# A four-layer vision block in one pass: layers and experts as two rows of pieces beside the scan, experts one at a time with their sum in DRAM, one PSUM ring for all

## The chip, the cores and the metric

The kernel runs on one core of a Trainium2 chip. The metric is the device time of one launch in microseconds (us); three runs of the kernel before gave 5811.77, 5817.92 and 5828.28 us, median 5817.92. The engines are called as in the profile: PE (TensorE, matmuls), PEld (its weight loads), DVE (VectorE), ACT (ScalarE), POOL (GpSimd) and SP (SyncE, which issues nearly all DMAs here).

## What is computed

The input `x` is 4 images of 384 channels by 48x48 positions, fp32. Four residual layers follow each other, each on a group-normalised input:

```
x = x + L0(_gn(x))   # Mamba block: projections, a 4-tap conv, a scan over 2304 positions
                     # with 768 channels x 16 states, gate, output projection, layer norm
x = x + L1(_gn(x))   # 1x1 projection, 8x8 FFT filter, 3x3 depthwise conv, gated GELU, 1x1 projection
x = x + L2(_gn(x))   # depthwise 11x11 convolution
x = x + L3(_gn(x))   # 4 experts (384->384->384, ReLU), outputs weighted by a coefficient per expert
```

In the last layer the coefficient of every expert is 1 for the given data unless some expert is never chosen. So the kernel sums all four experts unweighted, checks at the end, and recomputes with weights only if the check fails. This fallback (`weighted`) does not run here.

## The kernel before

**The scan.** `scans` is a generator. It walks 4 images (`b`) times 5 chunks (`t`) of 460 or 464 positions times 96 units (`q`), 1920 units in all. One unit handles 128 channels and one of the 16 states: ACT makes the decay `da` (L627, an Exp into PSUM), POOL makes `bu` (L631), DVE runs the recurrence (L635), DVE or POOL multiplies by the state's output row into `g` (L642), and PE turns `g` and adds it up in PSUM as `y` (L591). The output rows `bc` are broadcast from DRAM by an SP DMA for every second unit, into four buffers. The projections, the conv and the end of a chunk are planned at fixed units and take their PSUM tiles from `bank` of `scans`.

**Work beside the scan.** While image `b` is scanned, two lists of small closures, each with a weight, are worked off after every `yield`. `later(b - 1, bg)` is layers 1 to 3's gate scores of the previous image: layer 1 in strips (`patches`, `spectrum`, `taps`, `gelu`, `value`, `project1`), layer 2 by channel tile (`load2`, `blocks`, `windows`, `finish_band`), then `scores_of`. `experts(b - 2, pool, bg)` is layer 3 of the image before that. They stand in one queue, experts first, and a share of weight per unit is spent on it, so that it ends with the image.

**After the scan** there is a last part without a scan ("the tail" below): `later` of image 3, with the experts of image 2 interleaved piece by piece, then the routing (`route_all`), then the experts of image 3 alone.

**Experts.** `begin(e)` loads both weight matrices of an expert and scales the first; all four stay in SBUF. `biases` makes the bias corrections of all four. The steps go strip by strip (16 strips of 144 positions), and in a strip expert by expert, 64 per image. `hidden(s, e)` is 9 matmuls into PSUM (`ph`, L1142) and three ReLUs on ACT (`hr`, L1150); `output` is 9 matmuls (`pout`, L1160). `output` of step i-1 is placed behind `hidden` of step i. All four experts of a strip add up in one PSUM tile; DVE adds the input and the bias sum (L1171) and SP stores the strip.

**PSUM.** 8 banks. In the scan part: 2 for `bank` of `scans` (tag `mm`), 2 for `da`, 2 for `y`, and 2 single ones for the work beside it, tag `B` for nearly everything and `A` for sums that stay open (`dw`, `pc`, `pout`).

**Order.** Instructions are put in each engine's queue by a scheduler at build time, which takes them by their place in the program and by when it reckons them ready. On the chip each queue is worked off in order.

Of the kernel before, what the change touches and what calls it, by code (L numbers as in the profile page):

```python
# [16 lines left out]
P = 128  # L17
# [27 lines left out]
def tile_layers(ctx: ExitStack, tc: tile.TileContext, a: dict, out: bass.AP):  # L45
# [75 lines left out]
    def route_all(rt, bg):  # L121
# [44 lines left out]
        ps = bg.tile([P, 512], F32, name="pseen", tag="B")  # L166
# [97 lines left out]
    with ExitStack() as first:  # L264
# [55 lines left out]
        stats0 = wp.tile([P, NB, CT, 2, 3, 6], F32, name="stats0")  # L320
# [69 lines left out]
        stats1 = [wp.tile([P, CT, NC, 6], F32, name=f"stats1_{b}") for b in range(NB)]  # L390
        stats2 = [wp.tile([P, CT, NLB, 6], F32, name=f"stats2_{b}") for b in range(NB)]
        stats3 = [wp.tile([P, CT, len(BANDS), 6], F32, name=f"stats3_{b}") for b in range(NB)]
# [18 lines left out]
        def scans(wk, mm):  # L411


            def bank(name):
                return mm.tile([P, 512], F32, name=name, tag="mm")
# [5 lines left out]
            def image_stats(b, ct, h):  # L421
# [3 lines left out]
                for k in range(3):  # L425
                    nc.vector.bn_stats(stats0[:, b, ct, h, k, :], t[:, bass.ts(k, LB)])

            def image_norm(b):
                group_norm(
                    stats0[:, b].rearrange("p c h k s -> p c (h k) s"), bank,  # L430
                    mean0[:, b], rstd0[:, b], f"0_{b}",
                )
# [269 lines left out]
            def residual(i, ct):  # L702
# [14 lines left out]
                nc.vector.bn_stats(stats1[b][:, ct, t, :], x)  # L717
# [67 lines left out]
        def later(b, bg):  # L785
# [5 lines left out]
            def bank(name, tag="B"):  # L791
                return bg.tile([P, 512], F32, name=name, tag=tag)


            def begin1():
# [8 lines left out]
                group_norm(stats1[b], bank, mean, rstd, f"1_{b}")  # L804
# [27 lines left out]
            def patches(hb, wb):  # L832
# [10 lines left out]
                ts_ = d["ts"] = d["wk"].tile([P, C], F32, name=f"tp{u_}", tag="tp")  # L843
                nc.scalar.copy(ts_, ps[:, :C])

            def spectrum(hb, wb):
# [3 lines left out]
                us = d["wk"].tile([P, C], F32, name=f"uf{u_}", tag="uf")  # L850
# [21 lines left out]
            def taps(hb, ct):  # L872

                acc = d["acc", ct] = bank(f"dw{b}_{hb}_{ct}", "A")
# [11 lines left out]
            def gelu(hb, ct):  # L886
                if ct == 0:
                    d["act"] = d["wk"].tile([P, 2, LB], F32, name=f"act{b}_{hb}", tag="act")
# [13 lines left out]
            def project1(hb, ct):  # L902
# [11 lines left out]
                nc.vector.bn_stats(stats2[b][:, ct, hb, :], x)  # L914
# [31 lines left out]
            def begin2():  # L946
# [4 lines left out]
                group_norm(stats2[b], bank, mean, rstd, f"2_{b}")  # L951
# [11 lines left out]
            def load2(ct):  # L963
                x = d["x2", ct] = d["wk"].tile([P, HW], F32, name=f"x2_{b}_{ct}", tag="x2")
# [27 lines left out]
            def windows(ct, k, r, first, last):  # L992

                if first:
                    d["acc2"] = bank(f"pc{b}_{ct}_{k}", "A")
# [20 lines left out]
            def finish_band(ct, k):  # L1016
# [3 lines left out]
                nc.vector.bn_stats(stats3[b][:, ct, k, :], x)  # L1020
# [4 lines left out]
            work.append((1, lambda: load2(0)))  # L1025
# [331 lines left out]
```

## Time and profile before

| what | us |
|---|---|
| median of three runs | 5817.92 |
| profiled execution, its own time | 5822.38 |
| its span | 5820.6 |
| scan of image 0 (nothing beside it), first to next image's first unit | 981 |
| scan of image 1 (later) | 1171 |
| scan of image 2 (experts, then later) | 1352 |
| scan of image 3 (experts, then later) | 1322 |
| from the last scan instruction to the end of the span | 902 |

The four scan rows are the times between the first scan instructions (L635) of two images in the trace; image 3's ends with its last one. Busy time of an engine is the sum of its instructions' durations as the profiler shows them, merged where they overlap in the tables of stretches. PEclk is the share of full clock that PE was granted. The page's mean clock is 0.88.

### The profile page before, as it was taken

The numbers are of one execution on the slowest core, as the hardware profiler recorded it, in microseconds if no ns is written. First come the engines' busy times: TensorE is split into PE (matmuls) and PEld (weight loads), VectorE is DVE, ScalarE is ACT, GpSimd is POOL, SyncE is SP. The second block draws the span as 40 slices with busy tenths as digits, with TensorE's granted clock in tenths as the row PEclk, the third lists the DMA queues.
The fourth block names the chain that finished last, engine by engine and source line by source line (L and its number), as shares of the span: only waits on it lengthen the run. The fifth ranks groups of instructions, "written<-read, shape, count | busy, mean of one in ns | idle before, by whom it ended". The sixth has DMA issues, their size and how long they took to land. (4 is left out here: it accounts for less than half of the span.)

```text
span 5820.6 us, 78509 instructions
## 1 busy us (share of the span) xinstructions
PE 4897.0 (84%) x27796; PEld 3787.9 (65%) x27796; DVE 4014.5 (69%) x5653; ACT 3053.3 (52%) x6658; POOL 3110.4 (53%) x2795
## 2 busy tenths in 40 slices
PE   6677667778778898999867798999967698899999
PEld 3544444544456665889544676789744486789999
DVE  5888878889888787767788678666788767451110
ACT  3555555555566665555555576555555575345321
POOL 3877877765657677646464457555554556000000
PEclk9688778878789898999978699899978699899999
DMA  4344334333334335334333235333332334311100
GB/s 135 124 132 133 123 124 134 126 106 117 103 128 140 108 126 177 125 97 123 108 107 106 90 125 180 98 102 115 112 101 91 106 109 131 113 36 47 57 22 26
DMA packets 396048, 634.78 MB, mean 109 GB/s; under 512 B 32373, under 2 KB 386789, under 8 KB 392190
## 3 DMA queue, kind: packets, MB, share of 16 engines
q1 hardware_dynamic: 382148, 618.58, 33.5%
q10 hardware_dynamic: 13498, 11.11, 0.6%
q8 instruction: 220, 3.60, 0.3%
q14 instruction: 182, 1.49, 0.1%
HBM read 571.80 MB, written 57.80 MB: 108 GB/s over the span
## 5 line engine op out<-in xcount | busy, mean ns | idle before, releaser
L631 POOL TENSOR_TENSOR bu<-u,bc 128x460 f32<-128x460 f32 (+1 forms) x1920 | 2217.5, 1168 | 1348.8 <-DVE g L635 748.0
L591 PE MATMUL y<-ident,g 128*115 128x128 f32 (+1 forms) x7680 | 1346.3, 316 | 637.2 <-POOL g L642 539.8
L591 PEld LDWEIGHTS y<-ident,g 128*115 128x115 f32 (+1 forms) x7680 | 1110.5, 199 | 998.7 <-POOL g L642 686.2
L627 ACT ACTIVATE da<-dt,a_neg 128x460 f32<-128x460 f32 (+1 forms) x1920 | 1220.8, 645 | 667.3 <-DVE g L642 585.2
L635 DVE TENSOR_TENSOR_SCAN da<-da,carry,bu 128x460 f32<-128x460 f32 (+1 forms) x1008 | 1160.6, 1170 | 194.7 <-ACT da L627 155.6
L642 POOL TENSOR_TENSOR g<-g,bc 128x460 f32<-128x460 f32 (+1 forms) x660 | 765.9, 1160 | 268.2 <-DVE g L635 127.3
L642 DVE TENSOR_TENSOR g<-da,bc 128x460 f32<-128x460 f32 (+1 forms) x1260 | 771.1, 626 | 159.8 <-ACT carry L640 85.4
L635 DVE TENSOR_TENSOR_SCAN g<-da,carry,bu 128x460 f32<-128x460 f32 (+1 forms) x528 | 616.9, 1168 | 150.4 <-PE y L591 65.3
L1142 PE MATMUL ph<-xe,w 128*128 128x144 f32 x4608 | 624.8, 289 | 4.4 <-ACT hr L1150 3.9
L1160 PE MATMUL pout<-hr,w 128*128 128x144 f32 x4608 | 616.1, 287 | 0.0
L1142 PEld LDWEIGHTS ph<-xe,w 128*128 128x128 f32 x4608 | 591.1, 192 | 24.9 <-issue 10.9
L1160 PEld LDWEIGHTS pout<-hr,w 128*128 128x128 f32 x4608 | 584.8, 190 | 14.8 <-issue 7.9
L1001 PE MATMUL pc<-band,row 128*128 128x162 f32 (+14 forms) x3456 | 506.3, 297 | 3.8 <-DVE x L1019 3.5
L1001 PEld LDWEIGHTS pc<-band,row 128*128 128x128 f32 x3456 | 478.5, 205 | 20.9 <-DVE x L1019 6.9
L640 ACT COPY carry<-da 128x1 f32<-128x1 f32 x1008 | 158.7, 159 | 581.0 <-DVE da L635 575.9
L1150 ACT ACTIVATE hr<-ph,nb 128x144 f32<-128x144 f32 x768 | 235.6, 377 | 409.8 <-PE ph L1142 409.7
L881 DVE SCALAR_TENSOR_TENSOR dw<-pad,w_dw,dw 128x384 f32<-128x384 f32 x576 | 342.5, 610 | 12.9 <-ACT pad L869 9.3
L673 PE MATMUL po<-w_out,zs 128*115 128x384 f32 (+1 forms) x960 | 344.2, 500 | 4.3 <-DVE xc L504 3.5
L635 DVE TENSOR_TENSOR_SCAN da<-da,nil,bu 128x460 f32<-128x460 f32 x252 | 289.4, 1168 | 83.2 <-ACT da L627 65.9
L487 PE MATMUL pin<-xch,w_inx 128*128 128x463 f32 (+2 forms) x720 | 329.7, 586 | 7.6 <-DVE dt L582 5.4
L515 PE MATMUL pinz<-xch,w_inz 128*128 128x460 f32 (+1 forms) x720 | 317.9, 574 | 16.0 <-DVE xc L504 7.3
L1171 DVE SCALAR_TENSOR_TENSOR xe<-pout,b_sum,xe 128x144 f32<-128x144 f32 x192 | 58.7, 359 | 340.3 <-PE pout L1160 340.3
(173 smaller groups left out, 5355.6 us busy)
## 6 DMA issues: line engine op xcount, KB each, us to landing
bc<-bcd SPq DMA_DIRECT2D x768, 460.0 KB, 3.7
bc<-bcd SPq DMA_DIRECT2D x192, 464.0 KB, 3.6
xs<-x1d SPq DMA_DIRECT2D x24, 576.0 KB, 4.1
x2d<-xs SPq DMA_DIRECT2D x24, 576.0 KB, 3.0
x<-x2d SPq DMA_DIRECT2D x12, 1152.0 KB, 8.8
x3d<-x SPq DMA_DIRECT2D x12, 1152.0 KB, 4.6
xg<-x3d SPq DMA_DIRECT2D x24, 576.0 KB, 3.9
xe<-x3d SPq DMA_DIRECT2D x64, 216.0 KB, 2.6
```

The costliest lines, as they stand in the source:

```text
L487: nc.tensor.matmul(ps[:, lo : halo + n], lhsT=w_inx[:, k, bass.ts(j, P)], rhs=c["x"][:, k, lo : halo + n], start=k == 0, stop=k == CT - 1,)
L515: nc.tensor.matmul(ps[:, :n], lhsT=w_inz[:, k, bass.ts(j, P)], rhs=c["x"][:, k, DCONV - 1 : DCONV - 1 + n], start=k == 0, stop=k == CT - 1,)
L591: nc.tensor.matmul(y[:w, bass.ts(k, P)], lhsT=src[:, bass.ts(k, w)], rhs=ident, is_transpose=True, start=start and k == 0, stop=stop, skip ...
L627: nc.scalar.activation(da[:, :n], c["dt", p][:, m % 2, :n], AF.Exp, scale=a_neg[:, m, s : s + 1])
L631: nc.gpsimd.tensor_mul(bu[:, :n], c["u", p][:, m % 2, :n], bc[:, 0, :n])
L635: nc.vector.tensor_tensor_scan(here[:, :n], da[:, :n], bu[:, :n], last if t else nil[:, 0:1], ALU.mult, ALU.add,)
L642: eng.tensor_mul(g[:, :n], here[:, :n], bc[:, 1, :n])
L673: nc.tensor.matmul(ps[:w, :C], lhsT=c["zs"][:, m, bass.ts(k, w)], rhs=w_out0[:, m, :], start=m == 0, stop=m == MT - 1,)
L881: nc.vector.scalar_tensor_tensor(v, src, w_dw[:, ct, k : k + 1], v, ALU.mult, ALU.add)
L1001: nc.tensor.matmul(d["acc2"][:, : BANDS[k] * W].rearrange("p (h w) -> p h w", w=W)[:, lo - edges[k] : hi - edges[k], xlo:xhi], lhsT=d["row ...
L1142: nc.tensor.matmul(ps[:, bass.ts(m, EB)], lhsT=d["w1"][:, e, k, bass.ts(m, P)], rhs=d["x", s][:, k, :], start=k == 0, stop=k == CT - 1,)
L1160: nc.tensor.matmul(d["o"][:, bass.ts(m, EB)], lhsT=d["w2"][:, e, k, bass.ts(m, P)], rhs=d["h", s, e][:, k, :], start=e == 0 and m == 0 and ...
```

## The change

- **Two rows of pieces.** `later(b - 1)` is now worked off alone in the first three quarters of image `b`'s scan. When it is through, it appends `experts(b - 1)` to a second list, `two`, which is worked off at its own rate of one image's experts per image of scan. So experts start a quarter of a scan earlier, and run beside the layers of the next image instead of before them.
- **Experts one by one.** The loop is now expert by expert, and in an expert strip by strip. One expert's weights are in SBUF at a time (`bufs=1`), and its bias correction is made in `begin`. The sum over experts lies in a DRAM tensor `y3d`: expert 0 writes input, bias sum and its output there, experts 1 and 2 load the strip, add and store it, expert 3 loads it, adds and stores to `out`. The input strip is loaded again for each expert. `output(s, e)` now follows `hidden(s, e)` at once in the program, and `hr` has one buffer in place of three.
- **One PSUM ring.** `bank` of `scans`, of `later` and of `experts`, and now `pout` too, share one tag `mm` with 3 buffers in the scan part (6 in the tail); the open sums `dw` and `pc` have `acc` with 1 (2 in the tail).
- **Smaller buffers.** `tp`, `uf`, `act` and the layer-2 image tile `x2` go from 2 buffers to 1, and `load2` of the next channel tile is no longer issued ahead. Statistics are kept for 2 images in place of 4.

```diff
@@ experts: one at a time, sum in DRAM
+            y3d = dram.tile([C, HW], F32, name=f"y3d{b}")
...
+                w1 = d["w1"] = wk.tile([P, CT, C], F32, name=f"w1_{b}_{e}", tag="w1", bufs=1)
+                w2 = d["w2"] = wk.tile([P, CT, C], F32, name=f"w2_{b}_{e}", tag="w2", bufs=1)
...
+            def load3(s, e):
+                x = d["x", s, e] = wk.tile([P, CT, EB], F32, name=f"xe{b}_{s}_{e}", tag="xe")
                 nc.sync.dma_start(x, strip(x3d[b], bass.ts(s, EB)))
+                if e:
+                    y = d["y", s, e] = wk.tile([P, CT, EB], F32, name=f"ye{b}_{s}_{e}", tag="ye")
+                    nc.sync.dma_start(y, strip(y3d, bass.ts(s, EB)))
...
+                h = d["h"] = wk.tile([P, CT, EB], F32, name=f"hr{b}_{s}_{e}", tag="hr", bufs=1)
...
+                if e:
+                    y = d["y", s, e].rearrange("p c t -> p (c t)")
+                    nc.vector.tensor_add(y, ps[:, : CT * EB], y)
+                    to = strip(out[b] if e == NE - 1 else y3d, bass.ts(s, EB))
+                    nc.sync.dma_start(to, d["y", s, e])
+                    return
...
-            steps = [(s, e) for s in range(HW // EB) for e in range(NE)]
-            for i, (s, e) in enumerate(steps):
-                if e == 1 and s + 1 < HW // EB:
-                    work.append((0.2, lambda s=s: load3(s + 1)))
-                work.append((2.2, lambda s=s, e=e: hidden(s, e)))
-                if i:
-                    work.append((2.2, lambda i=i: output(*steps[i - 1])))
-            work.append((2.2, lambda: output(*steps[-1])))
+            for e in range(NE):
+                work.append((4, lambda e=e: begin(e)))
+                work.append((0.1, lambda e=e: load3(0, e)))
+                for s in range(NS):
+                    if s + 1 < NS:
+                        work.append((0.1, lambda s=s, e=e: load3(s + 1, e)))
+                    work.append((2.2, lambda s=s, e=e: hidden(s, e)))
+                    work.append((2.2, lambda s=s, e=e: output(s, e)))
@@ the scan part: two rows
+            banks[:] = mm, {"mm": 3, "acc": 1}
+            one, share, share2 = [], 0.0, 0.0
+            states = 2 * DS * (MT // 2) * NC
+            rate2 = None
             for b, t, q in scans(wk, mm):
                 at = 2 * DS * (MT // 2) * t + q
                 if b and at == 24:
+                    one, share = later(b - 1, banks), 0.0
+                    one.append((0, lambda b=b: two.extend(experts(b - 1, ew, banks))))
+                    rate = sum(w for w, _ in one) / (0.75 * (states - at))
+                share = run(one, share + rate) if one else 0.0
+                if two:
+                    rate2 = rate2 or sum(w for w, _ in two) / states
+                    share2 = run(two, share2 + rate2)
@@ the tail
+            banks[:] = mm, {"mm": 6, "acc": 2}
+            one, share = later(NB - 1, banks), 0.0
+            rate = sum(w for w, _ in two) / sum(w for w, _ in one)
+            for w, piece in one:
+                piece()
+                share = run(two, share + w * rate)
+            run(two, 1e9)
+            coef, whole = route_all(rt, mm)
+            run(experts(NB - 1, ew, banks), 1e9)
@@ layer 2: one image tile
-                x = d["x2", ct] = d["wk"].tile([P, HW], F32, name=f"x2_{b}_{ct}", tag="x2")
+                x = d["x2", ct] = d["wk"].tile([P, HW], F32, name=f"x2_{b}_{ct}", tag="x2", bufs=1)
...
-            work.append((1, lambda: load2(0)))
             for ct in range(CT):
-                if ct + 1 < CT:
-                    work.append((1, lambda ct=ct: load2(ct + 1)))
+                work.append((1, lambda ct=ct: load2(ct)))
```

`run(queue, share)` takes pieces from the front of a list as long as the share of weight covers the first one, and gives back what is left.

## The prediction

> **What bounds the kernel now.** I read first the busy shares, then the table of stretches cut where one kind of work beside the scan ends and the next begins, then the timeline of the tail.
>
> ```profile
> PE 4897.0 (84%) x27796; PEld 3787.9 (65%) x27796; DVE 4014.5 (69%) x5653; ACT 3053.3 (52%) x6658; POOL 3110.4 (53%) x2795
> ...
> 100.00:1074.00 974.00, 680.98 (x2903) 466.26 (x2902) 820.18 (x1022) 526.09 (x1115) 764.25 (x680) 0.78 0.41 128
> 1152.00:1657.00 505.00, 380.97 (x1490) 238.51 (x1489) 442.10 (x637) 275.56 (x575) 302.18 (x273) 0.81 0.36 109
> 1675.00:2180.00 505.00, 432.67 (x2452) 338.24 (x2453) 398.80 (x507) 334.69 (x728) 360.31 (x320) 0.88 0.39 128
> 2288.00:2788.00 500.00, 485.13 (x3454) 432.68 (x3453) 338.50 (x445) 264.68 (x662) 299.50 (x266) 0.98 0.36 111
> 2788.00:3253.00 465.00, 339.63 (x1326) 210.57 (x1325) 382.10 (x566) 243.51 (x491) 243.02 (x223) 0.81 0.34 105
> 3273.00:3561.00 288.00, 267.41 (x1746) 222.51 (x1745) 202.39 (x263) 205.24 (x413) 173.31 (x154) 0.93 0.35 116
> 4962.00:5240.00 278.00, 269.23 (x1677) 227.60 (x1678) 128.31 (x254) 107.62 (x220) 1.73 (x10) 0.94 0.23 75
> 5240.00:5500.00 260.00, 259.67 (x2122) 253.33 (x2123) 31.02 (x76) 123.57 (x310) 1.07 (x2) 1.00 0.14 47
> 5500.00:5821.00 321.00, 314.85 (x2476) 305.42 (x2474) 31.84 (x110) 63.91 (x203) 0.00 (x0) 0.98 0.11 31
> ```
>
> Columns: stretch, length, busy PE, PEld, DVE, ACT, POOL, PE's granted clock, DMA share, GB/s. In order: scan alone (image 0), layer 1 and layer 2 beside image 1's scan, experts, layer 1 and layer 2 beside image 2's scan, and the tail's three parts. Alone and under layer 1 the scan is bound by DVE (84%, 88%, 82%); under experts by PE (97%, DVE only 68%); under layer 2 mostly by PE (93%). The tail is PE from end to end. No row has both at 90%.
>
> ```profile
> 5600.80 2.37 PE L1142 MATMUL ph<-xe,w 128*128 128x144 f32 x18
> 5602.89 2.27 PEld L1160 LDWEIGHTS pout<-hr,w 128*128 128x128 f32 x18
> 5603.01 2.37 PE L1160 MATMUL pout<-hr,w 128*128 128x144 f32 x18
> 5603.27 0.92 ACT L1150 ACTIVATE hr<-ph,nb 128x144 f32<-128x144 f32 x3 [3.49 <-PE ph L1142]
> ...
> 5605.21 2.37 PE L1142 MATMUL ph<-xe,w 128*128 128x144 f32 x18
> ...
> 4918.23 0.57 ACT L1075 ACTIVATE sc<-pg,gb 4x384 f32<-4x384 f32 x1 [2.25 <-PE pg L1070]
> ...
> 4919.04 0.26 PEld L1079 LDWEIGHTS pgt<-ident,sc 4*128 4x128 f32 x3 [0.17 <-ACT sc L1075]
> ```
>
> One expert step is 5605.21 - 5600.80 = 4.41 us, without a gap: the `pout` at 5602.89 belongs to the step before, and covers the ReLUs that start at 5603.27.
>
> **Last image's experts** (5519 to 5820, all PE). In the built program's PE queue the `pout` of a step stands directly behind its own `ph` in all 64 steps of image 3; the scheduler pulls ahead at most one matmul of the next step. So PE waits for the first ReLU: its weight load would start at 5602.89, the ReLU starts at 5603.27 and takes 0.38, and ACT released PE at most 0.24 us after its end in the gate scores (last two lines: end 4918.80, PE 4919.04; 0.15 taken). 5603.27 + 0.38 + 0.15 - 5602.89 = 0.9. Ends: 0.5 (ReLU start and end taken from the matmul's modelled end, no wake-up) and 1.5 (all three ReLUs). The later two come 0.27 apart, while PE has 0.25 us pieces. 64 x 0.9 = **+58** (32 to 96).
>
> ```profile
> xe<-x3d SPq DMA_DIRECT2D x19, 216.0 KB, 2.5
> out<-xe SPq DMA_DIRECT2D x17, 216.0 KB, 2.1
> ...
> xg<-x3d SPq DMA_DIRECT2D x6, 576.0 KB, 3.8
> ```
>
> In expert 0 the strip `xe` is itself what is stored, and with two buffers the load two steps on waits for that store: add 1.0, store 2.1, load 2.5, wake-ups 0.4, together 6.0 against a step of 5.3. 16 x 0.7 = **+11** (0 to 30). Queued on SP behind it is only the next store. For experts 1 to 3 the input load waits only for `ph`, and `y3d` is loaded two steps ahead: hidden by the 5.3 us step, and no cost unless a load took twice its 2.5 us.
>
> With one buffer for the weights, `w1` of the next expert is loaded only after the last `ph` of this one: 0.2 wake-up + 3.8 (the row of equal size; 10.0 is the median where eight such loads were queued) + three scalings 1.6 (L1109, 3.14 for six) + 0.2, then bias matmuls of 2.7 (10.85 for four experts) before the next `ph`: 8.5 after the last one, 3.1 undisturbed. Three times 5.4 = **+16** (8 to 35). At the start, `pseen` (L167) now stands in PE's queue ahead of expert 0's bias matmuls; before, the biases of four experts and the first steps covered the routing on DVE. That chain ran from 5518.0 to 5541, of which 9.4 was waiting for the biases: 14 us. First `ph` then at about 5518 + 14 + 3 = 5535, before 5529.9: **+5** (-8 to +10). The whole bias cost of before, 10.8, is in this difference. Sum +90.
>
> **Layers of image 3 with experts of image 2** (4962 to 5519). By the built queue 15 of the 64 steps now lie ahead of the scan's end: 15 x 4.41 = -66, if PE stays full. Of the 49 left, 11 have `pout` right behind `ph` and 11 more under 1 us of other matmuls between: 11 x 0.9 + 11 x 0.5 = +15. Three expert starts, half covered by layer pieces: 3 x 2.7 = +8. In layer 1 (PEld 82% full) the steps also filled the waits between `pa`, `pf` and `pi`; a quarter fewer uncover 18 x 2 x 0.9 x 1/4 = +8. Sum **-35** (-66, nothing lost; 0, the steps had only filled gaps).
>
> **The scans.** More work: the steps' sums. Expert 0's three adds are 1.08 (L1171, 359 ns each); one add of 432 columns I take as 0.6, between 555 ns for 384 (L913) and 636 for 480 (L1019). 47 x 1.08 + 96 x 0.6 - 32 x 1.08 = 74 us of DVE. Per strip there are three more loads of the input, three loads and three stores of the sum: 9 x 216 KB x 16 = 32 MB per image, over 1300 us 25 GB/s on top of some 111; the stretch from 2245 to 2288 moves 219, so I cost the bytes at 0.
>
> Less waste: PE-bound experts spread over DVE-bound layers. I take needs per unit from the table, units being counted scan instructions (L635): DVE 820/477 = 1.72 us; PE (485 - 64 x 4.41)/186 = 1.09; layer 1 adds DVE 382 - 148 x 1.72 = 127; layer 2 adds PE 267 - 105 x 1.09 = 153 (124 in image 3; 140 taken) and DVE 21; the gate scores DVE 10. By the built queue layer 1 then spans 159 units, layer 2 167, the rest 154, with 64/480 step per unit at 0.72 us of DVE each (this holds the 74). Images 2 and 3: layer 1 DVE (273 + 127 + 15)/0.85 = 488, layer 2 PE (182 + 140 + 97)/0.95 = 441, rest DVE (265 + 10 + 15)/0.85 = 341, together 1270. The same sum for before gives 500 + 382/0.85 + 267/0.95 + 81/0.85 = 1325 (measured 1352 and 1322): -55 each. Image 1, with 15 steps at its end: 471 + 362 + 342 = 1175 against 520 + 480 + 152 = 1152, +23. Together -87. The ReLU waits are covered here by the 7.5 units, some 20 us, between two steps.
>
> Against it stand two prices that no row shows. `x2` with one buffer: store and load of 1152 KB (4.6 and 8.8 us to landing by the page) leave layer 2 without work for some 15 us, and by the built queue ACT then does four blocks in a row, 4 x (4 x 0.55 + 2 x 0.48) = 12.6 us without a `da`, whose two buffers last two units, about 5. Up to 7 us, twice per image in three scans: 0 to 45, I take 22. The ring: in a chunk's first 28 units the scan takes 21 tiles, layer 1 some 13, experts 7; 41 tiles on three banks in 78 us leave 5.7 us for each, and a `pin` alone needs three matmuls (0.59 each), an ACT pass and three DVE passes of some 0.6 beside 1.17 us scans. PE takes tiles in order, and behind one that waits stand the `y` transposes, which free `g` for DVE and POOL. From 0 to 143 steps x 2 tiles x one DVE scan (1.17) = 335; I take 4 us per chunk, 15 x 4 = 60, nearer to nothing because before had as many banks in sum. Scans: -87 + 22 + 60 = **-5** (-110 to +150).
>
> At nothing: `tp`, `uf` and `act` with one buffer (the next block's copy stands behind the matmul that reads the last; 0.9 per block, 0.9 x 18 per image, if not), the statistics, and SP: a store waits there for its add, with `bc` loads behind it, but these have four buffers, eight units or 22 us; only a later add would cost.
>
> [...]
>
> **Sum.** +90 - 35 - 5 = +50 on a profiled 5822 (span 5820.6 and 1.8 around it), which is 4.5 above the median; on the median 5818 that is 5868 us.
>
> **Rivals.**
> - *Interleaving wins (faster).* Ring and `x2` cost nothing: +90 - 35 - 87 = -32: 5786. For it: DVE at 68% in 981 us of experts. Against: it needs PE at 0.95 and DVE at 0.73 at once in layer 2; the best row, 0.97 and 0.68, has no more to give than a sum of 1.65. Chance 0.24.
> - *The change moves pieces and nothing else (no change).* The ReLU wait is 0.5 and starts are covered: 32 + 0 + 8 - 35 - 5 = 0: 5818. Chance 0.10.
> - *The shared ring stalls PE in the scan (clearly slower).* If each of 143 steps costs one bank wait of a DVE scan, 143 x 1.17 = 167 in place of 60: 5975. It decides from (87 - 22)/143 = 0.45 us per step on, where the scans begin to lose. For: DVE and ACT queues are in order, so an add waits behind 1.17 us scans. Against: steps are 7.5 units apart. Chance 0.18.
>
> The forecast has 0.48. Runs spread by 0.3% (5812 to 5828), so faster or slower means more than 17 us: faster 0.24, same 0.10, slower 0.66. The range goes a little beyond the faster rival and to the ring's: 5765 to 5975; the forecast's own is 5830 to 5910.
>
> **What would show it.** The gap between last `ph` weight load and first `pout` in the last 350 us (0.9 expected; step 5.3, expert 0's 6.0); first `ph` of image 3 some 15 us after the last score; 8.5 us between experts; scans of images 1, 2 and 3 near 1200, 1330 and 1300. It is wrong if the step stays at 4.4, or if scans 2 and 3 fall below 1280 each.

## The result and the profile after

The changed kernel takes 5945.1 us in the median of its runs (5943.3 to 5955.7), the kernel before 5816.4 (5811.8 to 5828.3): a ratio of 1.022 with a 95% interval of 1.020 to 1.024. The forecast was 5868 with a range of 5765 to 5975: the sign and the range held, but the change is +129 us where +50 was worked out.

First the busy shares of the changed kernel, from its page.

```profile
PE 4899.8 (82%) x27796; PEld 3827.4 (64%) x27796; DVE 4112.6 (69%) x5857; ACT 3049.8 (51%) x6656; POOL 3109.9 (52%) x2795
```

PE does the work it did before in the same busy time (4897.0 us then), DVE has 98 us more, and the span is 121 us longer. So the loss is idle time, and the question is where. The next table sums the stages of the two profiled executions. A scan is counted from the first scan instruction of an image to that of the next; the other bounds are the end of the last scan and the last score copy of image 3.

| stage, us | before | after | change | forecast |
|---|---|---|---|---|
| scan of image 0 | 981 | 961 | -20 | 0 |
| scans of images 1, 2, 3 | 1171, 1352, 1322 | 1217, 1338, 1288 | +47, -14, -34 | -5 together |
| layers of image 3 with experts of image 2 | 600 | 652 | **+52** | **-35** |
| experts of image 3 | 302 | 394 | +91 | +90 |
| span | 5820.6 | 5941.8 | +121 | +50 |

The scans gave more than forecast, the last image cost in sum what was forecast, and one stage went the other way. These are the stretches of the changed kernel after the scan: layer 1 of image 3, layer 2, scores, experts of image 3 (columns as in the prediction: stretch, length, busy PE, PEld, DVE, ACT, POOL, PE's granted clock, DMA share, GB/s).

```profile
4929.00:5223.00 294.00, 215.04 (x1113) 161.63 (x1113) 133.89 (x258) 90.17 (x166) 1.97 (x10) 0.85 0.27 78
5223.00:5508.00 285.00, 260.61 (x2055) 256.11 (x2054) 37.90 (x72) 118.23 (x297) 0.54 (x1) 0.93 0.31 88
5508.00:5548.00 40.00, 31.73 (x166) 18.62 (x164) 4.09 (x17) 6.21 (x15) 0.53 (x1) 0.87 0.53 166
5548.00:5942.00 394.00, 331.46 (x2396) 314.48 (x2396) 60.01 (x154) 66.34 (x206) 0.00 (x0) 0.94 0.41 111
```

Before, PE was busy from end to end here: 269 of 278 us in layer 1, 260 of 260 in the stretch after it. Now it idles 79 us in layer 1 and 24 in layer 2. Layer 1 is not shorter although it holds only 20 expert steps in place of 36.

What PE's weight loads waited for in layer 1 of the changed kernel (groups: line, engine, operation, shapes, count | busy, mean ns | idle just before them, and what ended it):

```profile
L1137 PEld LDWEIGHTS ph<-xe,w 128*128 128x128 f32 x378 | 53.6, 207 | 2.8 <-issue 1.8
L1153 PEld LDWEIGHTS pout<-hr,w 128*128 128x128 f32 x360 | 48.5, 196 | 11.8 <-ACT hr L1145 7.2 <-issue 2.2
L838 PEld LDWEIGHTS pa<-w_in,xn 128*128 128x128 f32 x108 | 23.2, 231 | 54.0 <-ACT xn L818 42.8 <-issue 4.8
L856 PEld LDWEIGHTS pi<-dft_i,uf 128*128 128x128 f32 x108 | 14.6, 206 | 24.0 <-DVE uf L853 24.0
...
L851 PEld LDWEIGHTS pf<-tp,dft_f 128*128 128x128 f32 x36 | 5.7, 196 | 14.2 <-ACT tp L846 14.2
```

The waits are those of layer 1's own chain: `pa` for the next strip's `xn` (54 us), `pf` for the copy `tp` (14), `pi` for `uf` (24; 18 pairs at 1.3). In the kernel before, steps stood in these gaps, and the same three groups waited 14.2, 4.4 and 1.0 us (layer 1 of image 3):

```profile
L836 PEld LDWEIGHTS pa<-w_in,xn 128*128 128x128 f32 x108 | 21.8, 216 | 14.2 <-ACT xn L816 4.1 <-issue 3.0 <-ACT w L1109 0.3
L854 PEld LDWEIGHTS pi<-dft_i,uf 128*128 128x128 f32 x108 | 14.6, 206 | 4.4 <-DVE uf L851 2.4
...
L849 PEld LDWEIGHTS pf<-tp,dft_f 128*128 128x128 f32 x36 | 5.6, 196 | 1.0
```

The timeline of one block of the changed kernel shows the gap (start, length, engine, line, operation, out<-in, in brackets the idle time and what ended it):

```profile
5021.55 0.91 PE L851 MATMUL pf<-tp,dft_f 128*128 128x384 f32 x2 [0.62 <-ACT tp L846]
5022.50 0.56 DVE L853 TENSOR_TENSOR uf<-pf,filt_t 128x384 f32<-128x384 f32 x1 [4.50 <-PE pf L851]
5023.11 0.74 PEld L856 LDWEIGHTS pi<-dft_i,uf 128*128 128x128 f32 x6 [1.26 <-DVE uf L853]
5023.11 0.94 PE L856 MATMUL pi<-dft_i,uf 128*128 128x128 f32 x6 [0.65 <-DVE uf L853]
5023.78 2.26 PEld L1137 LDWEIGHTS ph<-xe,w 128*128 128x128 f32 x18
```

PE waits 1.26 us for `uf`, and the whole `ph` of 18 matmuls that comes next, without a wait of its own, stands behind the gap and not in it. In the trace `pi` follows `pf` directly in 18 of 18 blocks; before, in 1 of 18, with six step matmuls between them in most others.

In layer 2 the loss is two gaps like this one, in which the next channel block is still on its way through the single `x2`:

```profile
5422.53 1.14 PEld L984 LDWEIGHTS pr<-ident,rep 128*128 128x128 f32 x6 [10.71 <-ACT rep L975]
```

In the last image a step has the form that was forecast: `ph`, then a wait for the first ReLU, then `pout`.

```profile
5793.79 0.93 ACT L1145 ACTIVATE hr<-ph,nb 128x144 f32<-128x144 f32 x3 [4.28 <-PE ph L1137]
5794.22 0.30 PEld L1153 LDWEIGHTS pout<-hr,w 128*128 128x128 f32 x2 [0.75 <-ACT hr L1145]
5794.23 0.51 PE L1153 MATMUL pout<-hr,w 128*128 128x144 f32 x2 [0.53 <-ACT hr L1145]
```

### The profile page after: what moved, and what is told of

It reads as the page before. It is cut to its first block, busy times and chain, and to the rows that moved or that the text cites. A ratio compares the mean times of both kernels' runs of the same rounds, so it can differ in the third digit from the quotient of the medians.

```text
span 5941.8 us, 80027 instructions
## 1 busy us (share of the span) xinstructions
PE 4899.8 (82%) x27796; PEld 3827.4 (64%) x27796; DVE 4112.6 (69%) x5857; ACT 3049.8 (51%) x6656; POOL 3109.9 (52%) x2795
## 5 line engine op out<-in xcount | busy, mean ns | idle before, releaser
L591 PE MATMUL y<-ident,g 128*115 128x128 f32 (+1 forms) x7680 | 1320.7, 312 | 626.9 <-POOL g L642 537.0
L591 PEld LDWEIGHTS y<-ident,g 128*115 128x115 f32 (+1 forms) x7680 | 1092.0, 196 | 970.2 <-POOL g L642 675.6
L1153 PE MATMUL pout<-hr,w 128*128 128x144 f32 x4608 | 693.5, 303 | 72.4 <-ACT hr L1145 70.9
L1153 PEld LDWEIGHTS pout<-hr,w 128*128 128x128 f32 x4608 | 637.7, 202 | 116.0 <-ACT hr L1145 94.9
L1137 PE MATMUL ph<-xe,w 128*128 128x144 f32 x4608 | 664.9, 295 | 7.4 <-DMA xe<-x3d 4.9
L1137 PEld LDWEIGHTS ph<-xe,w 128*128 128x128 f32 x4608 | 618.7, 198 | 25.7 <-issue 7.2
L1003 PE MATMUL pc<-band,row 128*128 128x162 f32 (+14 forms) x3456 | 484.9, 291 | 28.1 <-ACT row L992 27.6
L1162 DVE TENSOR_TENSOR ye<-pout,ye 128x432 f32<-128x432 f32 x192 | 115.6, 602 | 555.3 <-PE pout L1153 555.1
L1003 PEld LDWEIGHTS pc<-band,row 128*128 128x128 f32 x3456 | 461.5, 199 | 55.6 <-ACT row L992 36.6
L883 DVE SCALAR_TENSOR_TENSOR dw<-pad,w_dw,dw 128x384 f32<-128x384 f32 x576 | 343.0, 610 | 14.2 <-ACT pad L871 10.0
```

What stands on the lines that cost most here:

```text
L591: nc.tensor.matmul(y[:w, bass.ts(k, P)], lhsT=src[:, bass.ts(k, w)], rhs=ident, is_transpose=True, start=start and k == 0, stop=stop, skip ...
L883: nc.vector.scalar_tensor_tensor(v, src, w_dw[:, ct, k : k + 1], v, ALU.mult, ALU.add)
L1003: nc.tensor.matmul(d["acc2"][:, : BANDS[k] * W].rearrange("p (h w) -> p h w", w=W)[:, lo - edges[k] : hi - edges[k], xlo:xhi], lhsT=d["row ...
L1137: nc.tensor.matmul(ps[:, bass.ts(m, EB)], lhsT=d["w1"][:, k, bass.ts(m, P)], rhs=d["x", s, e][:, k, :], start=k == 0, stop=k == CT - 1,)
L1153: nc.tensor.matmul(ps[:, bass.ts(m, EB)], lhsT=d["w2"][:, k, bass.ts(m, P)], rhs=d["h"][:, k, :], start=k == 0, stop=k == CT - 1,)
```

## The experiments

Times are medians. Differences are against the kernel that was edited: the changed kernel's 5945.1, or the kernel before as it ran beside the experiment, 5815 to 5821. Stages come from one profiled execution: in the changed kernel and six runs that alter only what follows the scans, the scans ended between 4890 and 4907 us, so a difference of some 15 us in all the scans together says nothing. "The stage" is that of the layers of image 3. Where code is cut, "..." marks it.

**More steps into layer 1.** If layer 1 only lacked fillers, a higher rate gives them.

```
-            rate = sum(w for w, _ in two) / sum(w for w, _ in one)
+            rate = 1.8 * sum(w for w, _ in two) / sum(w for w, _ in one)
```

> The changed kernel, but after the scan the experts of image 2 advance 1.8 times as fast beside the layers of image 3, so that some 36 of the 49 steps left stand in layer 1, as before the change, in place of some 20. Nothing else is altered. Theory A (layer 1 after the scan is bound by its own chain from strip to strip; steps beside it only fill PE's waits, and the changed kernel puts too few there): layer 1 keeps its 277 us with PE busy 260 or more in place of 201, and layer 2 with the scores, 313 us now, loses 16 steps x 4.4 to 5.2 = 70 to 83; whole kernel 5862 to 5885. Rival B (the steps themselves bring the waits, through the ReLU that stands in PE's queue and the single buffers): what layer 2 loses layer 1 gains; 5930 to 5945. Rival C (no room in layer 1 for more, since one buffer for the hidden layer and one set of weights hold the steps back): layer 1's count stays below 28; 5905 to 5930.

Measured: 5926.6, -18. Layer 1 now holds 37 steps and takes 342 us in place of 293; layer 2 falls from 276 to 214. Of the 62 us that layer 2 loses layer 1 gains 49, as rival B had it in the main (the time is 3 us below its range), and theory A fell: with as many steps at hand as before the change, the waits before `pi` stay and those before `pa` shrink by a third only. Its weight loads' groups in layer 1:

```profile
L838 PEld LDWEIGHTS pa<-w_in,xn 128*128 128x128 f32 x108 | 22.4, 221 | 36.6 <-ACT xn L818 25.6 <-issue 3.6
L856 PEld LDWEIGHTS pi<-dft_i,uf 128*128 128x128 f32 x108 | 14.0, 198 | 22.8 <-DVE uf L853 22.8
```

`pi` waits 22.8 us, nearly the 24.0 of 20 steps. So what matters is not the number of steps but their place in PE's queue.

**Steps taken out of the kernel before.** Is the stage worth 4.41 us per step at all?

```
...
-            one, two = later(NB - 1, bg), experts(NB - 2, wk, xbg)
+            one, two = later(NB - 1, bg), experts(NB - 2, wk, xbg, HW // EB - 4)
```

> The kernel before, but for image 2 the experts handle 12 of 16 strips only: 48 of the 64 steps beside the layers of image 3; the outputs of four strips are left out. It measures by itself what taking steps out of that stage is worth. Working of the forecast (PE stays full): 16 x 4.41 = -71 from a stage of 600 us, whole kernel 5747. Theory A (layer 1 is bound by its own chain; only the steps that leave layer 2 count): layer 1 keeps 275 to 280 us with PE less busy, layer 2 and scores lose 7 to 12 steps, -30 to -53, whole kernel 5765 to 5787. Rival (the steps had only filled gaps everywhere): 0 to -15.

Measured: 5747.6, what the forecast's working gave (5747). Layer 1 keeps its 36 steps and 280 us, layer 2 goes from 233 to 166. So the -66 for 15 steps was a sound price, on the old queue. Theory A was wrong here too: layer 1 stays as full as it was, and all that is missing leaves layer 2.

**The ReLU wait, first attempt.** The output of a step goes behind the next step's hidden layer, with two buffers for the hidden layer.

```
-                h = d["h"] = wk.tile([P, CT, EB], F32, name=f"hr{b}_{s}_{e}", tag="hr", bufs=1)
+                h = d["h", s, e] = wk.tile([P, CT, EB], F32, name=f"hr{b}_{s}_{e}", tag="hr", bufs=2)
...
-                    work.append((2.2, lambda s=s, e=e: output(s, e)))
+                    if s:
+                        work.append((2.2, lambda s=s, e=e: output(s - 1, e)))
+                work.append((2.2, lambda e=e: output(NS - 1, e)))
```

> The changed kernel with two buffers for the hidden layer in place of one, and the output of a step placed behind the hidden layer of the next step, as before the change; one expert at a time and the sum in DRAM stay. If the ReLU wait is what a step of the last image lost: steps of 5.2 us go to 4.4 to 4.5 there, 60 x 0.75 = -45 in that stage, and the some 25 steps in layer 2 give another 10 to 20, while layer 1 gives nothing (theory A: there PE waits for the strips anyway); scans unchanged within 15; whole kernel 5880 to 5900. Rival B (in the layers' stage too the steps' ReLU waits are what was lost): another -20 to -35 in layer 1; 5850 to 5870. Rival D (the wait only changes its name: input strip, sum strip or ring end last instead): step above 4.9; 5920 to 5945.

Measured: 6059.5, +114, outside all that was expected. Steps of experts 1 to 3 of the last image do take 4.41 us, but a strip of expert 0 takes 11.7 to 13.5. Its timeline in expert 0:

```profile
5800.13 4.34 PEld L1137 LDWEIGHTS ph<-xe,w 128*128 128x128 f32 x18 [5.99 <-DMA xe<-x3d]
5800.14 4.69 PE L1137 MATMUL ph<-xe,w 128*128 128x144 f32 x18 [5.78 <-DMA xe<-x3d]
```

With only two `xe`, the load two strips on waits for a store that now stands a step later, and PE waits 6 us for it and then runs at half its rate (4.34 for 18 loads against 2.26). My edit moved the output and forgot the buffer that it frees. The scans lost 62 with it.

**The ReLU wait, with room for it.** The output again behind the next hidden layer, with three buffers for `xe`, `ye` and `hr`, for the last image alone.

```
...
+            with tc.tile_pool(name="last", bufs=2) as lw:
+                run(experts(NB - 1, lw, banks, 3, 3), 1e9)
```

> The changed kernel, but the experts of the last image have three buffers each for the input strip, the sum strip and the hidden layer, and a step's output stands behind the next step's hidden layer; one set of weights and the sum in DRAM stay; images 0 to 2 are untouched. The term of 58 for the ReLU wait and of 11 for expert 0's strips, taken away together: steps of 4.4 to 4.5 us in all four experts in place of 5.21 and 5.96; 60 x 0.78 + 15 x 0.75 = -58 and whole kernel 5882 to 5892. Starts of experts 1 to 3 stay, 7.5 to 10 us. Rival (the sum strip's round trip through DRAM is what paces a step once the ReLU is out of the way): steps 4.8 or more, 5905 or more.

Measured: 5886.1, -59; the last stage goes from 394 to 335 and the steps of experts 1 to 3 take 4.41. No `pout` waits for a ReLU any more. Expert 0 did not come down as expected: its steps take 5.35 us in the mean, since `ph` still waits up to 2 us for its input strip. Its timeline in expert 0 shows both:

```profile
5579.32 2.27 PEld L1137 LDWEIGHTS ph<-xe,w 128*128 128x128 f32 x18
5579.44 2.37 PE L1137 MATMUL ph<-xe,w 128*128 128x144 f32 x18
...
5581.53 2.27 PEld L1153 LDWEIGHTS pout<-hr,w 128*128 128x128 f32 x18
...
5585.46 2.26 PEld L1137 LDWEIGHTS ph<-xe,w 128*128 128x128 f32 x18 [1.66 <-DMA xe<-x3d]
```

**Starts of the experts.** Two sets of weights, fetched half an expert ahead, for the last image.

```
...
+                    if nw == 2 and s == 8 and e + 1 < NE:
+                        work.append((0, lambda e=e: fetch(e + 1)))
...
```

> The changed kernel, but the experts of the last image have two sets of weights, and those of the next expert are fetched while half of this one's strips are still to come; order, steps and routing stay. The forecast's term of 16 for three starts alone: the time from the last ph of an expert to the first of the next, 7.6 to 10 us, falls to about 6 (a step of 5.2, and the bias matmuls of 0.5 to 0.7); -8 to -13, whole kernel 5932 to 5937. Rival (scaling of the weights on ACT and the bias matmuls are the wait, the transfer is not): 0 to -4.

Measured: 5930.5, -15; the last stage goes from 394 to 375. A little more than the 8 to 13 expected; the three starts together give back 19 us.

**Two buffers for layer 2's block, after the scan.**

```
+                    [P, HW], F32, name=f"x2_{b}_{ct}", tag="x2", bufs=1 + (b == NB - 1)
...
+                elif ct + 1 < CT:
+                    work.append((1, lambda ct=ct: load2(ct + 1)))
```

> The changed kernel, but for image 3 the copy of a channel block in layer 2 has two buffers again and its load is issued a block ahead, as before the change; images 0 to 2 keep one buffer. The two gaps of 10.9 and 10.7 us before the transposes of layer 2 after the scan should go. If they are plain loss of PE: -20 to -24, whole kernel 5921 to 5925. Rival (steps of image 2 would have run in them, or the blocks' copies on ACT come late next): 0 to -8, 5937 to 5945.

Measured: 5924.1, -21: both gaps are gone and layer 2 takes 249 us in place of 276.

**Two buffers for every image**, with `row` at 11 buffers in the scans.

```
+                x = d["x2", ct] = d["wk"].tile([P, HW], F32, name=f"x2_{b}_{ct}", tag="x2")
...
+                        [P, NBC // 2, P], F32, name=f"row{v_}_{h}", tag="row", bufs=14 if b == NB - 1 else 11
...
+                if ct + 1 < CT:
+                    work.append((1, lambda ct=ct: load2(ct + 1)))
```

> The changed kernel, but layer 2's copy of a channel block has two buffers for every image, and its load is issued a block ahead, as before the change; in the scans the transposed rows have 11 buffers in place of 14 to make room. Undoing the single buffer alone in the kernel before showed +17, +12 and +17 in the scans of images 1 to 3. If it costs as much in the changed order: scans 1217, 1338 and 1287 fall by 35 to 50 together and the stage after the scan by 21 to 27; whole kernel 5870 to 5890. Rival (with the layers and the experts in two rows the scan has other work in the gap): scans within 12, whole kernel 5915 to 5925. Rival (11 rows are too few): scans longer.

Measured: 5911.0, -34, of which the scans have nothing: they end at 4899 us, as in the changed kernel (4896), and the stage goes from 652 to 624. So in the changed order the scans gain nothing from the second `x2`, as the first rival had it (the whole is 4 us below its range). The room for it came from three `row` buffers; whether these cost what it gave was not tried.

**One buffer in the kernel before.**

```
+                x = d["x2", ct] = d["wk"].tile([P, HW], F32, name=f"x2_{b}_{ct}", tag="x2", bufs=1)
...
+                work.append((1, lambda ct=ct: load2(ct)))
```

> The kernel before, with one part of the change alone: layer 2's copy of a channel block has one buffer and its load is issued only after the block before it was stored. Forecast's term: +22 in the scans of images 1 to 3 (bounds 0 to 45); after the scan the forecast had nothing, the changed kernel's trace shows two gaps of 10.9 and 10.7. Theory: +22 after the scan and +10 to +25 in the scans, whole kernel 5850 to 5867. Rival (in the scans the gap is filled by the scan itself): only the +22, 5838 to 5845; rival (after the scan the steps of image 2, with their own banks, fill the gaps): 5818 to 5840.

Measured: 5861.1, +46, all of it in the scans (1171, 1352 and 1322 become 1188, 1364 and 1339) and none after them: layer 2 takes 233 us as before. The total fits the theory and its parts do not. One buffer costs 46 us in one order, none that shows in the other, and after the scan 21 with the ring and nothing where the experts have banks of their own, as here.

**The ring in the scan, alone, in the kernel before.**

```
-                return mm.tile([P, 512], F32, name=name, tag="mm")
+                return mm.tile([P, 512], F32, name=name, tag="mm", bufs=3)
...
+                tag, n = ("mm", 3) if tag == "B" else ("acc", 1)
```

> The kernel before, with one part of the change alone: during the scan the passing tiles of the scan (two banks) and of the work beside it (one) share one ring of three. Order, experts and tail as before. Forecast's term: the ring costs some 60 us over the scans of images 1 to 3. Theory: scan of image 0, where nothing runs beside it, gains about 20 (981 to 961, as in the changed kernel), images 1 to 3 lose 10 to 25 each; whole kernel 5825 to 5880. Rival F (a third bank is worth as much to the scan under other work as alone, the ring costs nothing): images 1 to 3 gain too, whole kernel 5740 to 5800. Rival G (every step waits for a bank): images 2 and 3 lose 60 or more each; 5930 or more.

Measured: 5786.2, -29, in rival F's range: the four scans take 13, 13, 5 and 1 us less and end 34 us earlier (4884 for 4918). Under the work of the last images little of the gain is left.

**The ring in the scan undone, in the changed kernel.**

```
-                return mm.tile([P, 512], F32, name=name, tag="mm", bufs=3)
+                return mm.tile([P, 512], F32, name=name, tag="mm", bufs=2)
...
+                tag = "side" if "side" in banks[1] else "mm"
...
-            banks[:] = mm, {"mm": 3, "acc": 1}
+            banks[:] = mm, {"mm": 6, "side": 1, "acc": 1}
```

> The changed kernel, but during the scan its passing tiles have two banks and the work beside it one, as before the change; after the scan nothing is altered. Undoing it the other way round, in the kernel before, the shared ring gained 13, 13, 5 and 1 in the four scans. Theory (the ring helps the scan and costs nothing beside it): image 0 loses 15 to 20, the scans together 30 to 60, since in the changed order experts and layers pass 7 more tiles per step through the one bank at once; whole kernel 5975 to 6005. Rival (the forecast's term: a step's two tiles hold up the scan's): images 1 to 3 gain 40 or more together; 5890 to 5925.

Measured: 6019.8, +75; the scans become 981, 1242, 1342 and 1309 and end 69 us later (4965 for 4896). Against these banks the ring is worth 69 us in the scans of the changed kernel; the forecast charged 60 for it. They are not quite the banks of before: there `pout` shared bank `A` with the layers' sums, here it goes through the one bank `side` with `ph` and the layers. How much of the 69 is due to that was not tried.

**Banks of their own for the experts after the scan.** The ring of six there becomes two for the layers and four for the steps.

```
+                tag = "ex" if "ex" in banks[1] else "mm"
...
-            banks[:] = mm, {"mm": 6, "acc": 2}
+            banks[:] = mm, {"mm": 2, "acc": 2, "ex": 4}
```

> The changed kernel, but after the scan the expert steps get four PSUM banks of their own, and the layers two for passing tiles and two for sums, in place of one ring of six and two; the scan, all buffers in SBUF and the order of the pieces stay. In the built PE queue this brings matmuls of the steps back between every pf of layer 1 and its pi (17 of 18; none with the ring), and some 31 steps into layer 1 in place of 20. Theory E (the shared ring, whose banks pass in the order of the program, is what stiffened PE's queue after the scan, and so lost the fillers of layer 1): PE's gaps before pi fall from 24 us to below 5, those before pa by half or more, layer 1 stays at 275 to 295 us with 28 or more steps, layer 2 takes 8 to 11 fewer; the stage of 652 us goes to 595 to 615; whole kernel 5885 to 5910. Rival A (the strip chain, whoever stands between): gaps before pa and the stage within 15 us; 5930 to 5945. Rival (two banks are too few for the layers' passing tiles): layer 2 longer than 290; 5935 or more.

Measured: 5827.5, -118, beyond all that was expected (-35 to -60) and 0.2% from the kernel before (ratio 1.0021, 1.0008 to 1.0034). The stage falls from 652 to 550. Its stretches (layer 1, layer 2, scores):

```profile
4930.00:5218.00 288.00, 269.76 (x1629) 222.51 (x1628) 144.42 (x285) 104.40 (x213) 2.56 (x11) 0.96 0.41 120
5218.00:5410.00 192.00, 189.30 (x1533) 185.18 (x1533) 26.32 (x44) 103.80 (x252) 0.00 (x0) 0.99 0.23 70
5410.00:5446.00 36.00, 34.72 (x201) 22.46 (x200) 5.50 (x19) 7.70 (x18) 0.53 (x1) 0.95 0.66 208
```

The first stretch is 6 us shorter, but PE is busy 270 us in it and not 215, and 33 steps went through. (Layer 1 by itself, from its first load to its last sum, takes 272 us in place of 293.) A block of layer 1 now looks like this in the timeline:

```profile
5014.30 0.91 PE L851 MATMUL pf<-tp,dft_f 128*128 128x384 f32 x2
...
5014.73 1.00 PEld L1138 LDWEIGHTS ph<-xe,w 128*128 128x128 f32 x6
...
5015.25 0.56 DVE L853 TENSOR_TENSOR uf<-pf,filt_t 128x384 f32<-128x384 f32 x1 [0.19 <-PE pf L851]
5015.86 0.74 PEld L856 LDWEIGHTS pi<-dft_i,uf 128*128 128x128 f32 x6
```

Six matmuls of a step stand where PE had waited for `uf`; the idle time before `pi` falls from 24.0 to 3.3 us, before `pa` from 54.0 to 11.5, in the same groups:

```profile
L838 PEld LDWEIGHTS pa<-w_in,xn 128*128 128x128 f32 x108 | 19.0, 190 | 11.5 <-ACT xn L818 3.7
L856 PEld LDWEIGHTS pi<-dft_i,uf 128*128 128x128 f32 x108 | 13.5, 191 | 3.3 <-DVE uf L853 1.9
```

The gaps at `x2`, too, are filled by steps (idle before `pr` 1.1 us, 21.7 with the ring). And `pseen`, which in the ring stood ahead of expert 0's bias matmuls and held PE for 11.5 us, now holds it for 0.5: the last stage falls from 394 to 380.

**The same banks split the other way**, four for the layers and two for the steps: order against number.

> The changed kernel with banks apart after the scan, split the other way: the expert steps have two banks of their own and the layers four for passing tiles, in place of four and two. The built PE queue again has step matmuls between pf and pi (17 of 18). Theory (it is the order in one shared ring that cost the time, not how many banks either side has): the stage after the scan within 15 of 549 us, whole kernel 5820 to 5845. Rival (the experts needed four banks, the ring gave them too few): stage above 590, whole kernel 5870 or more.

Measured: 5838.7, with the stage at 551. The number of banks on each side is not it.

**The ring after the scan, alone, in the kernel before**: its two pairs for passing tiles become one ring of four.

```
+                tag, n = ("B", 4) if tag == "B" else (self.a, 2)
...
+            bg, xbg = Ring(bg), Ring(bg, "X")
```

> The kernel before, with one part of the change alone: after the scan the two pairs of banks for passing tiles (one of the layers, one of the experts) become one ring of four; the sums of both keep their own pairs. In the built PE queue pf and pi then stand side by side in 9 of 18 places (1 before), and 26 steps in place of 36 lie in layer 1. Theory (the shared ring stiffens the queue, whoever fills it): the stage of 600 us grows by half of what the changed kernel lost there, 30 to 60, whole kernel 5846 to 5880. Rival (only the changed step, with one buffer for the hidden layer, suffers from a ring): within 10, 5806 to 5826.

Measured: 5897.9, +79: the stage goes from 600 to 663, with 26 steps in layer 1, and the last image from 302 to 320. In 10 of 18 blocks `pi` follows `pf` directly. So the ring does it by itself, with the old step as well. The waits of the changed kernel come back, the one before `pi` by half, and so does the one for `pseen` (12.3 us). Its groups in layer 1 (all but the first four loads of `pa`):

```profile
L836 PEld LDWEIGHTS pa<-w_in,xn 128*128 128x128 f32 x104 | 23.5, 242 | 48.7 <-ACT xn L816 36.2 <-issue 6.7
L854 PEld LDWEIGHTS pi<-dft_i,uf 128*128 128x128 f32 x108 | 14.7, 206 | 13.0 <-DVE uf L851 12.5
```

**What paid, together**: the two rows and the ring in the scan, two `x2`, banks apart after the scan (two pairs for the steps), and for the last image the experts of the kernel before, all four summed in PSUM (`together` is that function under a new name).

```
...
+            banks[:] = mm, {"mm": 2, "acc": 2, "B": 2, "A": 2}
...
+            run(together(NB - 1, ow, mm), 1e9)
```

> What paid of both kernels together: the two rows of pieces in the scan and the shared ring there, two buffers for layer 2's block (11 for its rows in the scans), after the scan banks of their own for the experts of image 2, and for the last image the experts of the kernel before, all four summed in PSUM. By the parts: scan end 4895 - 45 = 4850, stage after it 600 - 51 = 549, last image 303, and 2 around the span: 5704 if all add up. If the single buffer's price does not come back in the scans: 5745 to 5755. Above 5790 the parts hinder one another.

Measured: 5738.6 (5727.3 to 5748.9), 0.986 of the kernel before with an interval of 0.984 to 0.988. That is 6 us below the range named for the case that the scans gain nothing from the second `x2`, and this case it is: they end at 4899. It is also 48 us less than the ring in the scan alone gave (5786.2). PE is full from layer 1 to the end (its stretches: layer 1, layer 2, experts of image 3):

```profile
4940.00:5230.00 290.00, 277.01 (x1667) 228.50 (x1667) 144.02 (x279) 104.56 (x215) 1.48 (x6) 0.95 0.45 135
5230.00:5407.00 177.00, 176.61 (x1458) 173.80 (x1457) 25.12 (x41) 102.67 (x247) 0.00 (x0) 1.00 0.21 65
...
5455.00:5747.00 292.00, 283.87 (x2301) 283.28 (x2300) 30.04 (x101) 59.65 (x194) 0.00 (x0) 0.99 0.09 24
```

## Why the prediction was right and wrong

**The failed step** is "Layers of image 3 with experts of image 2 ... -35". It took 15 x 4.41 = -66 "if PE stays full", and PE did not stay full. The ring was priced in the scans alone; in this stage it was not named, though the change puts layers and steps into one ring of six there. In the forecast's sum the waits between `pa`, `pf` and `pi` stood at +8, for a quarter fewer steps to fill them; their idle time went from 20 us to 92, +73. The single `x2` was priced in the scans only; here it opened two gaps of 10.9 and 10.7 us. Five runs settle the cause. The price per step was sound (48 of 64 steps in the kernel before: 5747.6 against the 5747 of that working). A higher rate in the same ring does not bring the fill back. Banks apart do, and then the stage is 50 us shorter than before, where the forecast had 35. Either split of the banks does it, and the ring alone, in the kernel before, costs 63 there. What the traces show of the way is the order in PE's queue: with one ring `pf` and `pi` stand side by side, with banks apart six step matmuls go between them. That a tile of the ring is had only in its turn, so that a step cannot be put ahead of a layer's tile whose turn is first, is how I read this order; the runs show the order and its price, not the planner's reasons. The +52 measured, then, is -50 for the rest of the change and +102 for the ring, which also kept steps out of the `x2` gaps.

**Last image's experts, +90**: measured +91, by the steps named, with sizes that made up for each other, which is luck. A step took 5.21 us for 4.41 (5.3 said): the ReLU wait is 0.80 per step and 51 in all, not 58. Expert 0's steps took 5.8 in the mean (6.0 said): 9 more, not 11. The three starts cost 25, not 16: beside the wait for the weights (the first four loads of `ph` came 5.1 to 6.3 us after the last ones of the expert before, the others only 7.8 to 9.3 us after them; 8.5 said), PE ran slower after it (the last 14 loads of each one's first `ph` took 3.42, 3.43 and 3.43 us, where a whole `ph` of 18 takes 2.26 in the running state), and the fetch ahead gave back 19. The first start cost 6 (5 said): the first `ph` came 17.7 us after the last score, before 11.7; the forecast's sum has 17 there, and its list of signs 15. `pseen` held PE for 11.5 us of it, and that wait is the ring's (0.5 with banks apart). The timeline of the changed kernel there:

```profile
5561.63 0.50 PEld L167 LDWEIGHTS pseen<-seen,ones 128*128 128x128 f32 x2 [11.45 <-DVE seen L161]
...
5562.01 3.96 PEld L1115 LDWEIGHTS pb<-mean,w 128*128 128x128 f32 x18
...
5565.85 4.39 PEld L1137 LDWEIGHTS ph<-xe,w 128*128 128x128 f32 x18
```

**The scans, -5**: measured -22, a sum near to the truth out of terms that were not; that is luck too. The ring, +60, is -69 in the changed order (and -34 in the old one): the scan gains a third bank, even alone (image 0, -20), and the waits behind a step that I feared do not outweigh it. `x2`, +22, shows nothing in the changed order (with three `row` buffers given up) and +46 in the old one. What is left for the interleaving, with the steps' sums, is -22 + 69 = +47 in place of -87: without the ring the scans end at 4965 us, before at 4918. (If `pout` in the one bank made the ring look better than it is, the interleaving looks worse by as much.) By images that is +72 for image 1, where 15 more steps are done, and -10 and -13 for images 2 and 3, where -55 each was worked out. The stages of image 2 in the changed kernel show where the sum was too kind. Layer 1, from its first `xn` to the first `rep` of layer 2, took 471 us where 488 were worked out; layer 2 took 482 in place of 441, and the rest (the image's first 93 us and the 291 behind layer 2) 384 in place of 341. The middles of the three:

```profile
2363.00:2815.00 452.00, 371.85 (x1885) 276.06 (x1886) 374.52 (x548) 240.47 (x528) 235.67 (x212) 0.87 0.42 126
2835.00:3312.00 477.00, 447.11 (x3013) 382.37 (x3012) 330.15 (x433) 306.98 (x721) 271.83 (x241) 0.96 0.47 141
3370.00:3600.00 230.00, 199.88 (x1232) 156.94 (x1231) 190.24 (x265) 120.33 (x221) 167.91 (x149) 0.96 0.54 157
```

In layer 2 PE is at 94%, as the sum had it (0.95), but it is busy for 450 us in the whole of it, where the sum had 419. In the rest DVE was busy for 305 us, where 290 were worked out, at 79% of the time and not 85%, with PE at 88% beside it. Over the whole image DVE was busy 1025 us, so the 1270 forecast needed 81%; it reached 77 (1025 of 1338), against 74 before (1000 of 1352). Why PE's work in layer 2 takes longer, and which wait keeps both engines below 90% in the rest, was not tried and stays open.

**The rivals.** "Interleaving wins" had its two free terms right (the ring and `x2` cost the scans nothing) and its gain wrong. "The shared ring stalls PE in the scan" named the right part of the change in the wrong stage and for the wrong reason: the time is lost after the scan, where PE waits for `uf` and `xn` with step matmuls behind the wait. "Nothing else than pieces moved" gave 5818, and with banks apart the change came to 5827.5; but that is no support for it, for there the last image still took 380 us in place of 302, and the stages ahead of it gave that back.

In the scans one more bank to rotate through gave 34 us in the old order and 69 in the changed one. After the scan six banks to rotate through, shared, lost 102 us against two and four apart, so the number of banks to rotate through does not say by itself who should share.

## What to carry to other kernels

Two kinds of work that are meant to fill each other's gaps can lose that when they draw from one rotating pool of buffers: look in the built queue at what stands between a producer and its consumer, for idle time beside work that could run may be a question of order and not of rate. A part of a change is priced in every stage that it touches; here a ring gave 69 us in one stage and took 102 in the next. And when one operation is moved behind another, count the buffers that its end sets free, not only those that it needs.

## What the runs showed of the hardware

Two long pauses of PE in the changed kernel cost more than their own length. After 9.50 us without a weight load the six `pa` matmuls of a block took 4.21 us, against 2.10 for the next blocks of the same kind; after the 11.45 us before `pseen` the 18 bias loads took 3.96 us, mostly 2.09 at earlier starts, and the first `ph` 4.39, against 2.26 in the running state. The 1.26 us before `pi` in the block shown above did not: its six loads took 0.74 us after them, and 0.74 also with banks apart, where a step left no gap. The `pa` rows from the changed kernel's timeline:

```profile
5010.06 4.21 PE L838 MATMUL pa<-w_in,xn 128*128 128x384 f32 x6 [8.36 <-ACT xn L818]
...
5018.83 2.10 PE L838 MATMUL pa<-w_in,xn 128*128 128x384 f32 x6
```

The granted clock of the stretch of layer 1 was 0.85 with the ring, where PE idled 79 of 294 us, and 0.96 with banks apart, where it idled 18 of 288.

That the scan of image 0, with nothing beside it, gained 20 us from a third bank, although DVE was 84% busy there, was not expected either. It came in every run with that bank (image 0 at 961 to 972 us) and in none without it (981 to 985).
